# A macaron block on one core: the first and last feed-forward nets in four parts, with weights multiplied ahead

## The chip, the cores and the metric

The kernel runs on one core of a Trainium2 chip. The metric is the device time of one launch, in microseconds (us). TensorE (PE) does products and transposes and has its weight loads listed apart (PEld); VectorE (DVE) and ScalarE (ACT) work on rows of 128 partitions; GpSimd (POOL) is a fourth engine; SyncE's queue (SP) and ScalarE's queue issue the transfers between DRAM and the on-chip memory. Products and transposes end in PSUM, the accumulator memory of eight banks.

## The reference

The input x has 8 chunks of 512 rows and 128 columns, float32. Three steps follow one another, with the same feed-forward weights in the first and the third:

```
x = x + 0.5 * ffn(norm(x))
x = x + attention(norm(x))        # 16 heads, Q and K of rank 64, softmax over 512 rows, VO 128x128 per head
x = x + 0.5 * ffn(norm(x))

def ffn(h):                       # three blocks k = 0, 1, 2
    y = gelu(norm(W1[k] h + b1[k]) * gamma[k] + beta[k])
    h = h + W2[k] y + b2[k]
W = (q / 7.5 - 1) * scale (one scale for 16 columns) + lora_b lora_a     # six matrices of 128x128
norm(v) = (v - mean) / sqrt(var + 1e-5)
```

Softmax runs along the keys, after division of the scores by the root of 128.

## The kernel before

The 512 rows of a chunk lie as four groups of 128 partitions. All matrices of the net are in SBUF, turned (wT). A planner holds the order: `at(t, fn)` files a task with a planned time, tasks are issued in order of that time, and each engine keeps this order exactly. The planned times are written out by hand; T0 is the planned start against the first scores at time 0.

The middle is 32 turns of about 32 us, each of two head pairs of one chunk. A turn computes scores (L624), row maxima (L631), exponentials (L636), the softmax's scaling on POOL and ACT (L648, L650), turns the weights by transposes in 32x32 tiles on DVE (L658) and transfers on SP, and adds the values (L694) into PSUM; projections (L562, L568) and values (L584) of later pairs and the blocks of the feed-forward nets of neighbouring chunks (`Unit`, `Block`: L286, L293, L311, L319, L325) lie between. Here `Norm` takes statistics on DVE (`bn_stats` L250, `bn_aggr` L252), the root on POOL in two instructions (add EPS L258, power −1/2 L259), and z on DVE (L264).

At the head and at the tail one chunk is alone: the first net of chunk 0 with its attention input before the first scores, and the second net of chunk 7 after the last values. `lay_parts` gives each two `Part`s of 256 rows. A part's block has a bias that a product writes to PSUM (L370), two 128-column products with wT (L378), Norm, two transposes (L235), gelu on ACT (L389), the second product (L397) and an addition to h on DVE (L403). HB = 5.5 is the planned time of a block and LAG = 2.55 the offset of the second part. Between the parts `busy` issues transposes that nobody reads (`warm`, L149): 18 at the start, 4 to 6 later, and so on; 12 ahead of the last turn's values, 18 at the tail's start. `lay_last_sum` turns the attention's result (L728, L734) and the last sum (L412) is stored in halves.

Before the head's blocks the loads (L105 to L124), the dequantising of six matrices (`Weights`, L181 to L213: two DVE instructions, the LoRA product and an addition on DVE, transposes and a copy), the columns of biases, gamma and beta (L164), and the transposes of Q and K for all eight pairs (L223) are done. One PSUM pool with banks by tag serves all of it (L66). `g0`, `g1`, `acc0`, `acc1` are one bank each, `scores` two pairs.

Of the kernel before, what the change touches and what calls it, by code (L numbers as in the profile page):

```python
# [18 lines left out]
def kernel(  # L19
# [46 lines left out]
    psum = ctx.enter_context(tc.tile_pool(name="psum", bufs=1, space=bass.MemoryType.PSUM))  # L66
# [9 lines left out]
    vecs = const.tile([P, D], F32, name="vecs")  # L76
    nc.gpsimd.memset(vecs, 0.0)
# [7 lines left out]
    def load_x(b):  # L85
        nc.sync.dma_start(out=xs[b], in_=x[b].rearrange("(p c) d -> p c d", c=NC))

    q_i = const.tile([P, NL, D], I32, name="q_i")
# [3 lines left out]
    la = const.tile([LR, NL, D], F32, name="la")  # L92
    lb = const.tile([P, NL, LR], F32, name="lb")
# [3 lines left out]

    groups = [(0, 2), (2, NL)]

    def load_q(l0, l1):  # L100
        nc.scalar.dma_start(
            out=q_i[:, l0:l1, :], in_=qweights.rearrange("l o d -> o l d")[:, l0:l1, :]
        )

    load_x(0)  # L105
    nc.scalar.dma_start(out=sc, in_=scales.rearrange("l o g -> o l g"))
    load_q(*groups[0])
    nc.sync.dma_start(out=lb, in_=lora_b.rearrange("l o r -> o l r"))
    nc.sync.dma_start(out=la, in_=lora_a.rearrange("l r d -> r l d"))
    load_q(*groups[1])  # L110
    nc.sync.dma_start(out=vecs[0:NL, :], in_=biases)
    nc.sync.dma_start(out=vecs[NL : NL + NB, :], in_=ln_gamma)
    nc.sync.dma_start(out=vecs[NL + NB : NL + 2 * NB, :], in_=ln_beta)
    nc.sync.dma_start(out=q_sb, in_=wq.rearrange("(g two) r d -> (two r) g d", two=2))
    nc.sync.dma_start(out=k_sb, in_=wk.rearrange("(g two) r d -> (two r) g d", two=2))
    nc.scalar.dma_start(
# [3 lines left out]
    load_x(1)  # L120
    load_x(2)
# [38 lines left out]
    cols = const.tile([P, NL + 2 * NB], F32, name="cols")  # L160
    ncol = NL + 2 * NB
    beta_at = NL + NB

    def columns():  # L164
        pt = bank("pt_cols", "g1")
        nc.tensor.transpose(pt[:, 0, :ncol], vecs[:ncol, :], ident[:ncol, :ncol])
        nc.scalar.copy(cols, pt[:, 0, :ncol])


    w = const.tile([P, NL, NG, GROUP], F32, name="w")  # L170
    wf = w.rearrange("p l g k -> p l (g k)")
    lbT = const.tile([LR, NL, P], F32, name="lbT")
    wT = const.tile([P, NL, P], F32, name="wT")

    class Weights:


        def __init__(self, l0, l1):
            self.l0, self.l1, self.n = l0, l1, l1 - l0

        def dequantized(self):  # L181
            l = slice(self.l0, self.l1)
            nc.vector.tensor_scalar(wf[:, l, :], q_i[:, l, :], 1.0 / 7.5, -1.0, ALU.mult, ALU.add)
            nc.vector.tensor_tensor(
                w[:, l], w[:, l],
                sc[:, l, :].unsqueeze(3).to_broadcast([P, self.n, NG, GROUP]), ALU.mult,
            )

        def lora_turn(self):
            self.pt = pt = bank(f"pt_lb{self.l0}", "acc1")  # L190
            for l in range(self.n):
                nc.tensor.transpose(pt[:LR, l, :], lb[:, self.l0 + l, :], ident)

        def lora_keep(self):
            nc.vector.tensor_copy(lbT[:, self.l0 : self.l1, :], self.pt[:LR, : self.n, :])

        def lora(self):
            self.pl = bank(f"pl{self.l0}", "acc1")
            for l in range(self.n):
                nc.tensor.matmul(  # L200
                    self.pl[:, l, :], lhsT=lbT[:, self.l0 + l, :], rhs=la[:, self.l0 + l, :],
                    start=True, stop=True,
                )

        def add(self):
            l = slice(self.l0, self.l1)
            nc.vector.tensor_tensor(wf[:, l, :], wf[:, l, :], self.pl[:, : self.n, :], ALU.add)

        def turn(self):
            pt = bank(f"pt_w{self.l0}", "acc1")  # L210
            for l in range(self.n):
                nc.tensor.transpose(pt[:, l, :], wf[:, self.l0 + l, :], ident)
            nc.scalar.copy(wT[:, self.l0 : self.l1, :], pt[:, : self.n, :])  # L213
# [5 lines left out]
    def projection_weights(src, dst, g0, scale, nm, t, t_keep):  # L219
        def turn():  # L220
            pt = bank(f"pt_{nm}{g0}", "acc1")
            for j in range(NC):
                nc.tensor.transpose(pt[:, j, :], src[:, g0 + j, :], ident)  # L223
            at_keep.append(pt)

        at_keep = []
        at(t, turn)
        at(t_keep, lambda: nc.scalar.mul(dst[:, g0 : g0 + NC, :], at_keep[0], scale))

    def transposed(src, name, tag):  # L230

        n = src.shape[1]
        p = bank(name, tag)
        for c in range(n):
            nc.tensor.transpose(p[:, c, :], src[:, c, :], ident)  # L235
        return p[:, :n, :]

    class Norm:
# [5 lines left out]
        def stats(self):  # L244

            n = self.n = self.src.shape[1]
            st = small.tile([P, NC, 6], F32, tag="st", name=f"st_{self.name}")
            self.mv = small.tile([P, NC, 2], F32, tag="mv", name=f"mv_{self.name}")
            for c in range(n):
                nc.vector.bn_stats(out=st[:, c, :], in_=self.src[:, c, :])  # L250
# [88 lines left out]
    class Part:  # L339
# [13 lines left out]
        def root(self):  # L353
            self.nm.root()
# [627 lines left out]
```

## Time and profile before

| what | us |
|---|---|
| median of three runs | 1098.97 |
| the runs | 1098.64, 1098.97, 1101.04 |
| the profiled execution, its span | 1102.69, 1100.9 |
| first scores (L624) | 35.95 |
| turn starts 0, 1, 2 | 35.95, 68.82, 103.35 |
| end of the last values (L694) | 1071.87 |
| last sum of x, end | 1098.07 |

The chain of waits follows the work that ended last back from the end, each piece with start, length and place; `issue` is time in which the engine waited for nothing visible; rows with ACTq or SPq are queue waits. Windows give the busy time of every engine in a stretch and the clock that the throttle granted to TensorE (1 is full). The profile's mean clock over the run is 0.996. POOL is busy 496.0 us and its adds of EPS take 9.6 us in all (42 with 4 columns, 228 ns each), the powers 128x2 713 ns and 128x4 1029 ns.

### The profile page before, as it was taken

How to read it: one execution, taken by the hardware profiler on the slowest of the kernel's cores; microseconds unless marked ns; L12 is line 12 of the kernel's file. 1: busy time of each engine (PE TensorE's matmuls, PEld its weight loads, DVE VectorE, ACT ScalarE, POOL GpSimd, SP SyncE). 2: the span in 40 equal slices, each digit the busy share in tenths (PEclk: the TensorE clock that was granted, in tenths of full speed). 3: DMA queues.
4: the chain of work that ended last, by engine and by line, in shares of the span. 5: the costliest groups of instructions: out<-in, count | busy, mean ns of one | idle time of the engine just before them, and what ended most of it. 6: DMA issues, size and time to landing. Idle time of an engine off the chain costs nothing.

```text
span 1100.9 us, 15782 instructions
## 1 busy us (share of the span) xinstructions
PE 1074.2 (98%) x4683; PEld 584.6 (53%) x4683; DVE 878.3 (80%) x1772; ACT 787.0 (71%) x1674; POOL 496.0 (45%) x427
## 2 busy tenths in 40 slices
PE   9889999999999999999999999999999999999987
PEld 7546544675555554555555455555445555554445
DVE  6788887878888898888889888888988887777725
ACT  2677787767777777777788777777777777777611
POOL 3453444445444455444445554444544444454402
PEclk9999999999999999999999999999999999999999
DMA  6066555665676545566655556755555665666640
GB/s 183 1 154 146 120 115 122 139 153 131 149 163 134 127 109 120 135 153 153 141 113 120 125 127 151 163 126 125 123 116 135 153 153 125 134 137 150 139 102 10
DMA packets 57291, 142.39 MB, mean 129 GB/s; under 512 B 18348, under 2 KB 22008, under 8 KB 57208
## 3 DMA queue, kind: packets, MB, share of 16 engines
q1 hardware_dynamic: 54840, 139.73, 56.5%
q10 hardware_dynamic: 2368, 1.66, 0.7%
q8 instruction: 39, 0.64, 0.3%
q14 instruction: 44, 0.36, 0.1%
HBM read 5.01 MB, written 2.10 MB: 6 GB/s over the span
## 4 chain that ended last, share of the span: by engine, by line
PE 80%; ACT 9%; DVE 7%; SPq 2%; issue 2%; DMA 1%; POOL 0%; DVEq 0%; ACTq 0%
PE acc L694 33%; PE ps L624 16%; PE pqk L562 9%; PE pv L584 8%; ACT e L636 4%; PE po L319 3%; PE py L286 3%; DVE nm L631 2%; DVE tr L658 2%; SPq L673 2%; PE p L235 2%; ACT e L650 1%; ACT L311 1%; PE warm_acc L149 1%; PE ph L235 1%
## 5 line engine op out<-in xcount | busy, mean ns | idle before, releaser
L648 POOL TENSOR_SCALAR e<-e,rden 128x512 f32<-128x512 f32 x256 | 398.6, 1567 | 331.0 <-DVE rden L643 330.9
L694 PE MATMUL acc<-eT,v 64*128 64x512 f32 (+1 forms) x1768 | 467.2, 590 | 2.3 <-DMA eT<-tr 1.2
L636 ACT ACTIVATE e<-ps,nm 128x512 f32<-128x512 f32 x512 | 345.2, 686 | 162.4 <-DVE nm L631 157.9
L658 DVE STREAM_TRANSPOSE tr<-e 128x1024 f32<-128x1024 f32 x256 | 312.9, 1231 | 34.2 <-POOL e L648 24.4
L631 DVE TENSOR_REDUCE nm<-ps 128x2 f32<-128x1024 f32 x256 | 299.6, 1207 | 50.7 <-PE ps L624 50.3
L694 PEld LDWEIGHTS acc<-eT,v 64*128 64x128 f32 (+1 forms) x1768 | 204.9, 188 | 213.8 <-issue 206.6
L624 PE MATMUL ps<-qk 64*128 64x512 f32 x1024 | 250.8, 599 | 3.4 <-ACT e L636 2.4
L650 ACT ACTIVATE e<-e,rden 128x512 f32<-128x512 f32 x256 | 177.0, 725 | 14.3 <-DVE rden L643 12.9
L624 PEld LDWEIGHTS ps<-qk 64*128 64x128 f32 x1024 | 99.1, 186 | 125.4 <-issue 84.4
L584 PE MATMUL pv<-vo_sb,axT 128*128 128x256 f32 x512 | 122.2, 381 | 0.0
L584 PEld LDWEIGHTS pv<-vo_sb,axT 128*128 128x128 f32 x512 | 95.5, 191 | 27.5 <-issue 14.4
L636 ACT ACTIVATION_READ_ACCUMULATOR e<-ps,nm 128x1 f32 x512 | 103.8, 203 | 0.0
L597 ACT COPY v<-pv 128x512 f32<-128x512 f32 x126 | 68.0, 596 | 47.5 <-PE pv L584 47.5
L258 POOL TENSOR_SCALAR rstd<-mv 128x4 f32<-128x4 f32 x42 | 9.6, 228 | 145.7 <-DVE mv L252 145.7
L643 DVE RECIPROCAL rden<-den 128x2 f32<-128x2 f32 x256 | 40.7, 162 | 36.0 <-ACT e L636 35.0
L562 PE MATMUL pqk<-axT,qT_w 128*128 128x512 f32 x124 | 64.0, 598 | 1.8 <-ACT e L636 1.8
L568 ACT COPY qk<-pqk 128x1024 f32<-128x1024 f32 x62 | 62.1, 1001 | 4.6 <-PE pqk L562 4.6
L562 PE MATMUL pqk<-axT,kT_w 128*128 128x512 f32 x124 | 63.3, 592 | 0.0
L325 DVE SCALAR_TENSOR_TENSOR hT<-po,cols,hT 128x512 f32<-128x512 f32 x42 | 31.0, 739 | 25.0 <-PE po L319 24.1
L286 PEld LDWEIGHTS py<-wT,hT 128*128 128x128 f32 x336 | 43.3, 194 | 13.5 <-DVE hT L325 6.6
L264 DVE TENSOR_SCALAR z<-y,mv,rstd 128x128 f32<-128x128 f32 x168 | 47.9, 354 | 2.1 <-POOL rstd L259 2.1
L293 DVE TENSOR_TENSOR y<-py,bias_bc 128x512 f32<-128x512 f32 x42 | 28.5, 680 | 25.6 <-PE py L286 25.5
(109 smaller groups left out, 769.0 us busy)
## 6 DMA issues: line engine op xcount, KB each, us to landing
eT<-tr SPq DMA_DIRECT2D x1016, 128.0 KB, 2.3
x<-in_L_attn_x_dram SPq DMA_DIRECT2D x8, 256.0 KB, 5.5
out_dram<-x SPq DMA_DIRECT2D x7, 256.0 KB, 2.5
eT<-tr ACTq DMA_DIRECT2D x8, 128.0 KB, 4.2
qk_sb<-in_L_attn_Q_dram SPq DMA_DIRECT2D x1, 512.0 KB, 4.3
qk_sb<-in_L_attn_K_dram SPq DMA_DIRECT2D x1, 512.0 KB, 5.6
q_i<-in_L_ffn_qweights_dram ACTq DMA_DIRECT2D x1, 256.0 KB, 4.8
out_dram<-x SPq DMA_DIRECT2D x2, 128.0 KB, 1.7
```

The costliest lines, as they stand in the source:

```text
L286: nc.tensor.matmul(self.py[:, c, :], lhsT=hTs[self.b][:, c, :], rhs=wT[:, 2 * self.k, :], start=True, stop=True,)
L562: nc.tensor.matmul(self.pg[:, i, :], lhsT=(qT_w, kT_w)[i][:, self.g, :], rhs=xTs[self.b], start=True, stop=True,)
L568: nc.scalar.copy(self.qk, self.pg)
L584: nc.tensor.matmul(p, lhsT=xTs[self.b][:, c, :], rhs=vo_sb[:, 2 * self.g : 2 * self.g + 2, :], start=True, stop=True,)
L597: nc.scalar.copy(self.v[:, c : c + NC // 2], self.pv[:, c : c + NC // 2])
L624: nc.tensor.matmul(ps[:, j, :], lhsT=self.qk[rows, 0, ts(c, P)], rhs=self.qk[rows, 1, :], start=True, stop=True,)
L631: nc.vector.tensor_reduce(self.nm[:, c, :], self.ps[c], AX.X, ALU.max, negate=True)
L636: nc.scalar.activation(e[:, j, :], self.ps[c][:, j, :], AF.Exp, bias=self.nm[:, c, j : j + 1], accum_out=self.den[:, c, j : j + 1],)
L648: nc.gpsimd.tensor_scalar(e, e, r, None, ALU.mult)
L650: nc.scalar.activation(e, e, AF.Copy, scale=r)
L658: nc.vector.transpose(self.tr[:, :, :, c, :], self.e[c].rearrange("p h (k j r) -> p j (h k) r", j=Q4, r=32),)
L694: nc.tensor.matmul(accs[self.b][i], lhsT=self.v[rows, k, j, :], rhs=self.eT[rows, :, j * NC + k, :], start=first, stop=end and (j == 1 or ...
```

## The change

The two ends are laid out anew; the plan of the middle is the same except where named.

- **PSUM** comes from three pools in turn, "start", "attention" and "end". In the ends each of the four parts has a bank of its own for the sums of its three blocks and the final one (`y0` to `y3`), and a quarter of a bank for transposes.
- **Four parts** of 128 rows replace two of 256. Biases enter PSUM by transposing a broadcast column. Statistics of each part are a `bn_stats` and a `bn_aggr` whose input holds a constant third entry D·EPS, so the root is one POOL instruction; the middle's Norm uses the same form.
- **Weights multiplied ahead**: W1[k]·W2[m] is made once (`natural`, `multiplied`), so the pre-activation of block k is a sum in PSUM of W1[k]·h0, and of products with the earlier blocks' gelu outputs. In the tail no second product, no h and no addition remain between blocks; in the head the first block keeps them (`second`, `second_add`), and later ones don't. `constants` puts the earlier blocks' biases in.
- **`busy` transposes**: left are 14 at the start and eight at each of four places of turn 0 (times 5.3, 10.4, 15.6, 31.9); those between the parts, the 12 before the last values and the 18 at the tail's start are gone.
- **Weights**: scale first divided by 7.5 (`sc75`), then one DVE instruction for dequantising; LoRA is added in PSUM by TensorE.
- **Loads** come in another order and in pieces, over both queues. Q and K of pair 0 are turned at the head; pairs 1 to 3 and 4 to 7 in turn 0, along with two of the multiplied weights. The Exp table is loaded at time 0.01, after the first scores, and the eight `busy` before turn 1 use bank acc0.
- **Rings**: y two instead of three buffers (the attention copy `a` shares them), aT two instead of three in Block, hT three instead of four.
- **The last stores** are four, one a part, on SP and ACT.

```diff
-    psum = ctx.enter_context(tc.tile_pool(name="psum", bufs=1, space=bass.MemoryType.PSUM))
+    class Psum:
+        def __init__(self):
+            self.names, self.stack = ["start", "attention", "end"], ExitStack()
+        def next(self):
+            self.stack.close()
+            self.tile = self.stack.enter_context(tc.tile_pool(
+                name=f"psum_{self.names.pop(0)}", bufs=1, space=bass.MemoryType.PSUM,
+                reuse_waits="tile",
+            )).tile
...
+    sts = const.tile([P, 6, NC, 9], F32, name="sts")
+    nc.gpsimd.memset(sts, 0.0)
+    nc.gpsimd.memset(sts[:, :, :, 8:9], D * EPS)
...
+    load_lb(0)
+    load_q(0, 1, nc.scalar)
+    load_x(0, 0, 2)
     nc.scalar.dma_start(out=sc, in_=scales.rearrange("l o g -> o l g"))
+    load_la(0, nc.scalar)
+    nc.sync.dma_start(out=bias_rows, in_=biases)
+    load_x(0, 2, NC)
+    load_q(1, G, nc.scalar)
+    load_lb(1)
+    nc.sync.dma_start(out=gb_rows[0:NB, :], in_=ln_gamma)
+    nc.sync.dma_start(out=gb_rows[NB : 2 * NB, :], in_=ln_beta)
+    load_la(1, nc.sync)
+    load_q(G, NL, nc.sync)
+    load_projections(0, 1)
+    load_x(1)
+    load_projections(1, HP)
+    load_x(2)
...
+    def dequantized(l0, l1):
+        i, n = l0 // G, l1 - l0
+        nc.vector.scalar_tensor_tensor(
+            w[i][:, l0 - G * i : l1 - G * i],
+            q_i[:, l0:l1, :].rearrange("p l (g k) -> p l g k", k=GROUP), -7.5,
+            sc75[:, l0:l1, :].unsqueeze(3).to_broadcast([P, n, NG, GROUP]), ALU.add, ALU.mult,
+        )
...
+    def weights(l0, l1, tag):
+        i, n = l0 // G, l1 - l0
+        pt = bank(f"pt_w{l0}", tag)
+        for l in range(n):
+            nc.tensor.matmul(
+                pt[:, l, :], lhsT=w[i].rearrange("p l g k -> p l (g k)")[:, l0 - G * i + l, :],
+                rhs=ident, is_transpose=True, start=l == 0, stop=False,
+            )
+        for l in range(n):
+            nc.tensor.matmul(
+                pt[:, l, :], lhsT=la[i][:, l0 - G * i + l, :], rhs=lbT[i][:, l0 - G * i + l, :],
+                start=False, stop=l == n - 1,
+            )
+        return lambda: nc.scalar.copy(wT[:, l0:l1, :], pt[:, :n, :])
...
+    def natural(m, tag):
+        pt = bank(f"pt_nat{m}", tag)
+        nc.tensor.transpose(pt[:, 0, :], wT[:, 2 * m + 1, :], ident)
+        return lambda: nc.scalar.copy(nat[:, m, :], pt[:, 0, :])
+    def multiplied(ks, m, tag):
+        pt = bank(f"pt_x{ks[0]}{m}", tag)
+        x = const.tile([P, len(ks), P], F32, name=f"wx{ks[0]}{m}")
+        for i, k in enumerate(ks):
+            nc.tensor.matmul(
+                pt[:, i, :], lhsT=nat[:, m, :], rhs=wT[:, 2 * k, :], start=True, stop=True
+            )
+            wX[k, m] = x[:, i, :]
+        return lambda: nc.scalar.copy(x, pt[:, : len(ks), :])
...
+        for i, (k, m) in enumerate(((2, 1), (1, 0), (2, 0))):
+            nc.tensor.matmul(
+                pt[:, 0, i : i + 1], lhsT=wT[:, 2 * k, :], rhs=col[2 * m + 1],
+                start=i == 0, stop=i == 2,
+            )
...
-            st = small.tile([P, NC, 6], F32, tag="st", name=f"st_{self.name}")
+            norms.append(self.name)
+            st = sts[:, NC + len(norms) % 2]
...
-            nc.gpsimd.tensor_scalar(rstd[:, :n], self.mv[:, :n, 1], EPS, None, ALU.add)
-            nc.gpsimd.tensor_tensor(rstd[:, :n], rstd[:, :n], mhalf[:, :n], ALU.pow)
+            nc.gpsimd.tensor_tensor(rstd[:, :n], self.mv[:, :n, 1], mhalf[:, :n], ALU.pow)
...
-            y = work.tile([P, NC, D], F32, tag="y", name=f"y{self.name}")
+            y = work.tile([P, NC, D], F32, tag="y", name=f"y{self.name}", bufs=2)
...
-            self.aT = work.tile([P, NC, P], F32, tag="aT", name=f"aT{self.name}")
+            self.aT = work.tile([P, NC, P], F32, tag="aT", name=f"aT{self.name}", bufs=2)
...
-        hTs[b] = work.tile([P, NC, P], F32, tag="hT", name=f"hT{f}_{b}", bufs=4)
+        hTs[b] = work.tile([P, NC, P], F32, tag="hT", name=f"hT{f}_{b}", bufs=3)
...
+        def stats(self, k=None):
+            self.src = self.x() if k is None else self.y[:, k, :]
+            nc.vector.bn_stats(out=sts[:, self.c, 0, 0:6], in_=self.src)
+        def mean(self):
+            self.mv = small.tile([P, 2], F32, tag="pmv", name=f"pmv{self.name}")
+            nc.vector.bn_aggr(out=self.mv, in_=sts[:, self.c, 0, :])
         def root(self):
+            self.rstd = small.tile([P, 1], F32, tag="prstd", name=f"prstd{self.name}")
+            nc.gpsimd.tensor_tensor(self.rstd, self.mv[:, 1:2], mhalf[:, 0:1], ALU.pow)
...
+        def to_y(self, k, lhsT, rhs, end=False, turn=None):
+            nc.tensor.matmul(
+                self.y[:, k, :] if isinstance(k, int) else self.y[:, k[0] : k[1], :],
+                lhsT=lhsT, rhs=rhs, is_transpose=turn, start=bool(k == 0 and turn), stop=end,
+                skip_group_check=True,
+            )
         def bias(self, k):
+            b = col[2 * k] if k <= self.known else consts[self.known][k]
+            self.to_y(k, b.to_broadcast([P, P]), ident, turn=True)
+        def input(self, k, k1=None):
+            if k == NB:
+                self.to_y(k, self.h, ident, turn=True)
+            elif k1 is None:
+                self.to_y(k, self.h, wT[:, 2 * k, :], end=k <= self.known)
+            else:
+                self.to_y((k, k1), self.h, wT[:, 2 * k : 2 * k1 - 1 : 2, :])
+        def of_block(self, k, m):
+            self.to_y(
+                k, self.g[m], wX[k, m] if k < NB else wT[:, 2 * m + 1, :],
+                end=m == min(k, NB) - 1,
...
+        def second(self, k):
             nc.tensor.matmul(
+                self.p[1], lhsT=wT[:, 2 * k + 1, :], rhs=self.g[k], start=True, stop=True
+            )
+        def second_add(self, k):
+            h = self.h
             nc.vector.scalar_tensor_tensor(
+                self.new_h(), self.p[1], col[2 * k + 1], h, ALU.add, ALU.add
...
+    def part_banks(f):
+        ys = [bank(f"py{f}_{i}", f"y{i}") for i in range(NC)]
+        p = [bank(f"pp{f}_{i}", f"g{i}") for i in range(2)]
+        return [(ys[i], [p[i % 2][:, 2 * (i // 2) + j, :] for j in range(2)]) for i in range(NC)]
...
-        a.append(work.tile([P, T], F32, tag="a", name=f"a{b}", bufs=1))
+        a.append(work.tile([P, T], F32, tag="y", name=f"a{b}", bufs=2))
...
-    T0 = -33.0
...
+    T0 = -23.98
+    t = {k: T0 + v for k, v in START.items() if isinstance(v, float)}
     at(T0 + 0.1, table, AF.Gelu)
     at(T0 + 1.4, idle_bank, "acc0")
+    at(T0 + 1.5, busy, 14)
...
+        (t["qt"], t["qtk"], q_sb, qT_w, 0, 1, 1.0 / math.sqrt(D), "acc0"),
+        (t["kt"], t["ktk"], k_sb, kT_w, 0, 1, 1.0, "acc1"),
+        (0.4, 0.6, q_sb, qT_w, 1, 4, 1.0 / math.sqrt(D), "acc1"),
+        (1.4, 1.5, k_sb, kT_w, 1, 4, 1.0, "g1"),
+        (20.0, 24.3, q_sb, qT_w, 4, HP, 1.0 / math.sqrt(D), "acc1"),
+        (24.6, 28.4, k_sb, kT_w, 4, HP, 1.0, "acc1"),
+    ):
+        projection_weights(src, dst, g0, g1, scale, tag, ta, tb)
+    lay(20.1, 24.2, natural, 0, "acc0")
+    lay(24.5, 28.3, multiplied, (1, 2), 0, "acc0")
...
+    at(0.0, psum.next)
+    at(0.01, table, AF.Exp)
+    at(0.3, idle_bank, "acc0")
+    at(31.8, idle_bank, "acc0")
+    for t in (5.3, 10.4, 15.6, 31.9):
         at(t, busy, 8)
...
-    at(t + 25.8, idle_bank, "scores")
-    at(t + 25.9, busy, 12)
...
-    at(E + 1.65, idle_bank, "acc1")
-    at(E + 1.7, busy, 18)
...
+    for m in lay_parts(1, B - 1, 0, E, END, end_banks, (
+        ("xadd", "attended"), ("start", "start"), ("y0", "input", 0), ("in12", "input", 1, NB),
+        ("y1", "of_block", 1, 0), ("o20", "of_block", 2, 0), ("y2", "of_block", 2, 1),
+        ("in3", "input", 3), ("o30", "of_block", 3, 0), ("o31", "of_block", 3, 1),
+        ("o32", "of_block", 3, 2),
+    )):
```

## The prediction, made before the result was known

> **What bounds the kernel now.** I read the section of busy shares first, then the chain of waits over the whole span, then its pieces at both ends, then windows for the granted clock.
>
> ```profile
> PE 1074.2 (98%) x4683; PEld 584.6 (53%) x4683; DVE 878.3 (80%) x1772; ACT 787.0 (71%) x1674; POOL 496.0 (45%) x427
> PE 80%; ACT 9%; DVE 7%; SPq 2%; issue 2%; DMA 1%; POOL 0%; DVEq 0%; ACTq 0%
> ```
>
> TensorE bounds the middle: the 32 turns run from the first scores (L624, 35.95) to the end of the last L694 (1071.87). At the ends its 98% is misleading, because fillers (L149) count as busy. The ends hold 35.95 + (1100.9 − 1071.87 = 29.0) = 65 us, in which one chunk's feed-forward net runs with nothing beside it. So the change must be read from the ends, and from what it leaves in the turns.
>
> ```profile
> 1086.41 0.57 ACT aT L389
> 1086.98 0.04 issue
> 1087.02 0.70 PE po L397 x2
> 1087.72 0.43 PE py L370 x2
> 1088.15 0.22 PE warm_acc L149 x2
> 1088.37 0.64 PE py L378 x4
> 1089.01 0.27 PE p_b L235 x2
> 1089.28 0.02 issue
> 1089.30 0.02 ACTq L389
> 1089.32 0.05 issue
> 1089.36 0.57 ACT aT L389
> 1089.94 0.04 issue
> 1089.98 0.70 PE po L397 x2
> ...
> 1097.17 0.45 PE ph L235 x2
> 1097.63 0.02 issue
> 1097.65 0.42 DVE x L412
> ```
>
> The chain of waits, tail: two halves alternate, 2.96 us each, so a block takes 5.92. Of each 2.96 TensorE works 2.26 in its written order (second product, bias, filler, first product, the other half's transposes) and waits 0.70 for the gelu. The root on POOL is covered by the other half. The last sum ends at 1098.07, 26.2 after the last L694; the store and the span's end take 2.83 more.
>
> ```profile
> 43.49:46.90 3.41, 1.57 (x9) 0.58 (x6) 2.75 (x4) 2.86 (x7) 2.80 (x3) 1.00 0.02 5
> 46.90:50.31 3.41, 3.41 (x13) 2.94 (x14) 3.12 (x7) 1.14 (x4) 2.52 (x2) 0.50 0.00 0
> 60.55:63.97 3.42, 1.65 (x6) 0.75 (x5) 3.42 (x5) 2.79 (x8) 0.61 (x2) 1.00 0.80 175
> 1057.25:1060.66 3.41, 1.25 (x7) 0.70 (x7) 1.61 (x10) 0.00 (x0) 1.26 (x2) 1.00 0.16 35
> 1060.66:1064.07 3.41, 3.41 (x15) 2.89 (x14) 0.00 (x0) 0.78 (x1) 0.00 (x0) 0.50 0.00 0
> ```
>
> Windows: length, busy PE, PEld, DVE, ACT, POOL, then the clock. The clock's edges lie 3.41 us apart or a multiple of it (5.94, 46.90, 50.31, 1060.66, 1064.07). The step after one with TensorE 1.57 (46%) or 1.25 us busy (37%) ran at half clock; 60.55, with 1.65 (48%), kept the full clock after it.
>
> **The change, part by part.** I laid the instructions of both ends, old and new, on each engine in its written order with the durations of the rows (below: the adding-up): product of 128 columns 0.38 alone (0.215 each in a row); transpose 0.33; statistics 0.28 and their mean 0.15; pow 128x2 0.71 and 128x4 1.03, so 128x1 about 0.55 (by extension); z 0.34; ACT copy 256 0.37 and 512 0.59, so 128 about 0.27; gelu 256 0.56 and 512 0.78, so 128 about 0.46; sums 256 0.42, so 128 about 0.31; handover 0.02 to 0.04, to POOL 0.08.
>
> *Tail.* From block 0 on, second product (0.70), its add (0.50), bias (0.43) and fillers leave the chain; the EPS add on POOL (0.23) too. One part needs per block: product 0.38, statistics 0.43, handover 0.08, pow 0.55, z 0.34, transpose 0.33, gelu 0.46, handovers 0.25 = 2.8. Four parts share VectorE, which per block does 4 x (0.28 + 0.15 + 0.34) = 3.1 us. The larger decides: 3.2 against 5.92. Before the blocks: copy of the result 0.27, transpose with the 16 bias transposes among them (16 x 0.107 = 1.7, beside VectorE), then four parts through x add, statistics, mean, z at 1.05 each: the last z ends about 5.0 after L694, transpose, copy and product bring its first pre-activation to 6.2. Three periods of 3.2 less the product already counted, the last product 0.43 and sum 0.31: 6.2 + 9.6 + 0.7 = 16.4. The same adding-up of the old tail gives 24.3 where the rows have 26.2, so I stretch by 1.08: 17.7. The store (a quarter of the rows, on its own queue) stays at 2.8. Gain 8.5. Bounds: if the parts' sharing is as bad as today's halves (TensorE in its order), the period is 4.0 and the gain 6.1; if the plan holds unstretched, 10.
>
> *Head.* The first pre-activation cannot start before scales, weights, LoRA and x. Old row: 8.78. New: LoRA-B first, 14 warmers at the half clock end 4.7, its three transposes to 5.8, copy, W0, copy: 7.8. The landings of the new order are unseen; nearest rows are x0 3.73, scales 4.14, lb 5.11, la 5.85, so 7.5 to 9.3; I take 7.8. ACT issues four loads (0.5 each) ahead of its table load, which ends at 4.1, before its first copy. On SP, Q and K of pair 0 stand behind the last three weights; their transposes come at 10.0 in TensorE's order, where the old Q landed at 9.76 and K at 11.5: 0 to 1.5, I take 0, since a piece is an eighth of a load. Chunk 1's x (old 12.2) is first read at 22. Block 0 is slowed by turning five more weights between (TensorE 10.0 to 12.0 waits twice for an ACT copy of wT, 0.5 each) and keeps its second product; then blocks of 3.3. The last sum of x comes at 22.1 by this adding-up. There the order hurts: chunk 1's four statistics and means (1.07 on VectorE) and its 128x4 pow (1.03 on POOL) are ahead of the last part's root, and its z is at 25.9 instead of 23.5. Transpose 0.33, copy 0.27, K product and the remaining Q: scores at 27.8. The same adding-up gives 33.5 for the old 35.95; gain 5.7 x 1.07 = 6.0. From 21 to 26 TensorE is busy 42 to 44% of any 3.4 us by the same adding-up, below the 46% at which the clock fell, so I expect the next 3.4 us at half clock: projections and first scores (1.15 alone at full) cost 1.0 more (0 to 2). Net 5.0. Bounds 2 and 9 (the plan's own order without chunk 1's insertion, 2.4 better).
>
> *The first two turns.* Five further Q/K weight transposes and two sets in turn 0: 0.5 on TensorE. The Exp table (1.28, L142) now comes after the last copies and largely fits under scores 1.15 + maximum 1.24; 0.3 is left. The eight warmers before turn 1 use bank acc0 and wait for the copy of the last multiplied weights, behind v copies on ACT: 1.6. Turn 1 had 0.6 of issue (70.83) waiting for eT, absorbed by a later start. Sum +1.8 (0.5 to 4).
>
> *The last turn.* Twelve fillers (2.49 at half clock) go; eT had landed at about 1058.8, so L694 starts after the transposes of 1059.70 (x4). The stretch at half clock follows the hole anyway. I take −1.3 (0 to −2.5).
>
> *Turns 2 to 30.* One instruction less per Norm (L258, 0.23 on POOL, which waits 145.7 us for its inputs and mostly off the chain), smaller rings for y, aT, hT. Nothing on TensorE changes. Cover: TensorE is busy 98%; without it each of 42 roots would give 0.3. I take 0, bounds −3 and +3.
>
> Sum against the profiled execution's 1102.69: −8.5 − 5.0 + 1.8 − 1.3 = −13.0, 1089.7. The three runs' median is 3.7 lower, so 1086.0.
>
> **A rule that speaks against it.** The rows above put the edge between 46 and 48% of a step. The Trainium skill, "TensorE: Matmul & The Clock Gate", Part 1, says the clock halves after an idle free-running window of 3413 ns; the trace's steps agree in length, but its windows were not idle. Its Part 4 says that the full clock does not engage for transposes; here the first 18 fillers are transposes and the clock was full from 5.94, so the trace decides. By Part 4's rule the bare tail, with half its TensorE work transposes, would lose the clock often: an estimate from that page is 4 us more, 1090.
>
> **The rivals.**
> *Clock lost in the ends (about 1091).* If two steps of the tail and one more of the head run at half clock, products and transposes on the chain (0.38 + 0.33 per 2.8 us) take twice as long and the four parts queue on TensorE: about 1.7 a step, 5 more. For it: short records with waits between them; how much of a record counts as work is unseen. Against: by the same adding-up the tail keeps TensorE at 75% or more, until its last sums.
> *The head gains nothing (about 1091).* If scales or the last three weights land 2 us late, or the turn-0 work grows to 4, only the tail's 8.5 less the extras is left.
> *The order holds as planned (about 1081).* Chunk 1's root falls elsewhere and no clock is lost: 4 to 5 better.
> *Slower than before (about 1104).* Rings of two y (shared with the attention copy), two aT, three hT: a bias add on VectorE (L293) that waits for a ring's old reader stands before the row maxima, and so before the exponentials. It decides from 13/31 = 0.42 us a turn; at 0.6 a turn it is +18.6 − 13, +5.6. For it: VectorE is 80% busy. Against: TensorE's idle time before L624 and L694 is 3.4 and 2.3 us in all, and DVE's waits for POOL 24.4.
> *The ends stay under another bound (no change, 1098).* The old tail's chain has no DMA in it, so I see no cover.
>
> **How the numbers follow.** Forecast 0.58; clock 0.14; head without gain 0.11; order as planned 0.09; slower 0.06; no change 0.02. The likeliest gives 1086.0. Its bounds by terms, mostly independent, are about ±4; the two weaker cases reach 1092, the better 1081. Range 1080.5 to 1092.5. A measurement of this kernel tells 0.2% (2.2 us) from no change: faster 0.92, same 0.02, slower 0.06.
>
> **What would show it.** Right: first scores near 29, last sum about 18 after the last attention product, part blocks about 3.3 apart; turn 1 starting about 35 after turn 0; a granted clock of 0.5 around the first scores; 30 middle turns within 0.05 us of before. Wrong: block period near 4 or a tail at half clock; the first pre-activation after 9; a wait in every turn for y or hT.

## The result, and the profile after

The changed kernel takes 1086.23 us (median of four runs, 1085.0 to 1087.01) beside 1099.11 for the kernel before (four runs); the ratio of the runs is 0.9878, with a 95% interval of 0.9861 to 0.9896 (the two medians give 0.9883). The forecast was 1086.0. The profiled execution took 1085.0, its span is 1083.2.

The stages of the two profiled executions, from the first scores' start, the starts of each turn's first row maximum, the end of the last values and the span's end (from the first scores to the first row maximum both take 1.18, which no row holds):

| stage | before | after | difference | forecast |
|---|---|---|---|---|
| to the first scores | 35.95 | 29.58 | −6.4 | −5.0 |
| turns 0 and 1 | 67.40 | 68.33 | +0.9 | +1.8 |
| turns 2 to 30 | 916.7 | 915.8 | −0.9 | 0 |
| last turn, to the end of the values | 50.63 | 48.28 | −2.35 | −1.3 |
| tail | 29.0 | 20.06 | −8.9 | −8.5 |
| span | 1100.9 | 1083.2 | −17.7 | −13.0 |

The spans differ by 17.7, the medians by 12.9. The profiled execution of before was 3.6 above its median, that of after 1.2 below. Of this scatter 1.2 lies in turns 3, 5, 6 and 23, which had 0.2 to 0.4 more in the one profile of before and show both values in later profiles of its variants (turn 3 31.38 and 31.03, turn 23 33.29 and 32.94). Turn 0 may hold another 0.9: it took 33.27 in the one profile of before, 32.31 and 32.45 in two variants of it with the same head and turn 0. Where the rest lies was not found. So the total agrees to 0.2 us, but the terms below add up to 4.7 more than the forecast, and its carry-over from profile to median hid that.

Section 1 of the page of after, the busy shares:

```profile
PE 1061.0 (98%) x4630; PEld 563.4 (52%) x4630; DVE 874.5 (81%) x1765; ACT 795.0 (73%) x1710; POOL 484.5 (45%) x367
```

Nothing here tells the gain: TensorE has the same share, and only 53 instructions less. The chain of waits does. The tail of after, with start, length and piece:

```profile
1063.19 0.28 ACT oT L1103
...
1068.30 0.28 ACT ph L469
1068.57 0.04 issue
1068.61 1.15 PE py L473 x6
1069.76 0.41 PE pp L462 x2
...
1079.16 1.11 PE py L473 x6
...
1080.29 0.29 DVE end L523
```

Where TensorE waited 0.70 of each 2.96 us for a gelu, there is one unbroken run of TensorE from 1068.61 to 1080.27. Each piece is products and transposes of whichever part is due; no gelu, root or addition stands in the chain. The first part's gelus start at 1069.91, 1073.49 and 1076.86: a block takes 3.4 to 3.6, where it took 5.92. The last sum ends 17.4 after the last values (before 26.2).

The head's end in after, the same view:

```profile
23.63 0.29 DVE x L523
23.93 0.78 DVE sts L336 x4
24.70 0.30 DVE mv_n L338 x4
...
25.87 1.01 POOL rstd_n L344
26.88 0.52 POOL prstd L453
...
27.43 0.36 DVE pz L457
```

L336, L338 and L344 are chunk 1's statistics and root; they stand on VectorE and on POOL ahead of the last part of chunk 0, whose z (L457) is the last thing the projections need.

### The profile page after: what moved, and what is told of

Read it like the earlier page. It is cut to its first block, busy times and chain, and to the rows that moved or that the text cites. A ratio compares the mean times of both kernels' runs of the same rounds, so it can differ in the third digit from the quotient of the medians.

```text
span 1083.2 us, 15632 instructions
## 1 busy us (share of the span) xinstructions
PE 1061.0 (98%) x4630; PEld 563.4 (52%) x4630; DVE 874.5 (81%) x1765; ACT 795.0 (73%) x1710; POOL 484.5 (45%) x367
## 4 chain that ended last, share of the span: by engine, by line
PE 79%; ACT 9%; DVE 8%; issue 2%; SPq 1%; POOL 1%; DMA 0%; DVEq 0%; ACTq 0%; POOLq 0%
PE acc L792 33%; PE ps L722 16%; PE pv L682 9%; PE pqk L659 8%; ACT e L734 5%; PE po L403 4%; DVE tr L756 3%; PE py L371 3%; DVE nm L729 3%; PE py L473 2%; PE p L318 2%; SPq L771 1%; ACT e L748 1%; ACT L396 1%; ACT v L695 1%
## 5 line engine op out<-in xcount | busy, mean ns | idle before, releaser
L792 PEld LDWEIGHTS acc<-eT,v 64*128 64x128 f32 (+1 forms) x1768 | 196.9, 188 | 219.1 <-issue 216.5
L722 PEld LDWEIGHTS ps<-qk 64*128 64x128 f32 x1024 | 94.6, 186 | 127.9 <-issue 89.9
L344 POOL TENSOR_TENSOR rstd<-mv,mhalf 128x4 f32<-128x4 f32 x42 | 43.0, 1024 | 150.9 <-DVE mv L338 150.9
L695 ACT COPY v<-pv 128x512 f32<-128x512 f32 x126 | 68.0, 596 | 46.9 <-PE pv L682 46.8
```

Source lines behind the costliest of these rows:

```text
L695: nc.scalar.copy(self.v[:, c : c + NC // 2], self.pv[:, c : c + NC // 2])
L722: nc.tensor.matmul(ps[:, j, :], lhsT=self.qk[rows, 0, ts(c, P)], rhs=self.qk[rows, 1, :], start=True, stop=True,)
L792: nc.tensor.matmul(accs[self.b][i], lhsT=self.v[rows, k, j, :], rhs=self.eT[rows, :, j * NC + k, :], start=first, stop=end and (j == 1 or ...
```

## The experiments

All ratios are to the kernel before, run beside each; 0.9878 is the changed kernel's. Beside the experiments the kernel before took 1100.3 to 1100.7 (medians of 9 to 19 runs), 1.2 to 1.6 above its 1099.11 beside the changed kernel, which was not run again. So a ratio compared with 0.9878 can be off by 0.001 to 0.0015 from this alone, and what a part is worth is read from the stages of the profiles. In what follows a step is one of the stretches of 3.41 us at whose ends the granted clock can change, and a half step is one at half clock.

### Chunk 1's statistics earlier

```diff
-    m.lay_start((-3.3, -2.9, -1.6, 1.95, 3.7), "g0")
+    m.lay_start((-13.05, -13.0, -1.6, 1.95, 3.7), "g0")
```

> The changed kernel with chunk 1's statistics and root planned at -13.05 and -13.0 instead of -3.3 and -2.9, so that they no longer stand before the last part's root. Theory (the insertion costs the head its place): in the changed kernel the last part's z starts at 27.43, after 1.2 us of chunk 1's statistics on VectorE and 1.01 us of its power on POOL; without them 25.0, so first scores 29.6 - 2.3 = 27.3 and the time 2 us shorter (1 to 2.5), less what the moved 1.2 us on VectorE cost block 1 of the parts (0 to 0.5). Rival (TensorE or ACT is the bound there anyway): first scores move less than 0.5.

Ratio 0.9853 (0.9821 to 0.9886), which overlaps the changed kernel's interval; three runs took 1080.91 to 1083.17, one 1089.31. The last z starts at 25.76 instead of 27.43 and the first scores at 27.96 instead of 29.58. So the insertion cost the head 1.6 us. 2.3 was expected; 0.4 of the difference is that the parts' last sum came later (24.06 instead of 23.63), and the clock also rose 0.4 later (5.28 instead of 4.85).

### Q and K of pairs 1 to 3 turned in the head

```diff
-        (0.4, 0.6, q_sb, qT_w, 1, 4, 1.0 / math.sqrt(D), "acc1"),
-        (1.4, 1.5, k_sb, kT_w, 1, 4, 1.0, "g1"),
+        (T0 + 20.5, T0 + 20.6, q_sb, qT_w, 1, 4, 1.0 / math.sqrt(D), "acc0"),
+        (T0 + 20.7, T0 + 20.8, k_sb, kT_w, 1, 4, 1.0, "acc1"),
```

> The changed kernel with the Q and K transposes of pairs 1 to 3 and their copies at 20.5 to 20.8 of the head's plan instead of behind the first scores. Theory (turn 0 lost 1.1 us to them): in the changed kernel ACT's copy of K waits for transposes queued behind the second scores and the first exponentials start at 33.15, 1.16 after the maximum they need ended; then turn 0 gets shorter by 1.1 and the first scores stay at 29.6 (0 to 0.3 later). Rival (turn 0 is bound by chunk 1's first block or the values): turn 0 shorter by less than 0.4.

What it was about, in the timeline of after (start, length, engine, line, work, and the idle time before it with what ended it):

```profile
30.76 1.23 DVE L729 TENSOR_REDUCE nm<-ps 128x2 f32<-128x1024 f32 x1 [0.88 <-PE ps L722]
...
32.18 0.55 PE L308 MATMUL pt_g<-ident,qk_sb 128*128 128x128 f32 x3
...
32.76 0.49 ACT L311 ACTIVATE kT_w<-pt_g 128x384 f32<-128x384 f32 x1 [0.70 <-PE pt_g L308]
33.15 0.68 ACT L734 ACTIVATE e<-ps,nm 128x512 f32<-128x512 f32 x1
```

The maximum is ready at 31.99. The first exponential stands behind a copy that stands behind transposes that stand behind the second scores: 1.16 us lost, and not by the Exp table, which had ended at 31.46. With the transposes moved the exponential starts with the maximum's end:

```profile
34.16 0.69 ACT L734 ACTIVATE e<-ps,nm 128x512 f32<-128x512 f32 x1 [0.34 <-DVE nm L729]
```

Turn 0 is 33.43; the fair comparison is the profile with chunk 1's statistics moved, 34.55, since both ran it at full clock: 1.1 shorter, as expected. The ratio is 0.9835 (0.9816 to 0.9854). The median moved by more than 1.1 (1082.51 against 1086.23). The mean granted clock of the four executions is 1.000, that of the changed kernel's 0.997 to 0.998, so the half steps of after are missing here; whether the move or chance kept them out is not shown. And this profiled execution began late: its first scores are at 31.73, for a reason that the run with fillers in the holes shows.

### The tail of before in the changed kernel

```diff
-    at(E + 0.01, psum.next)
...
-    for m in lay_parts(1, B - 1, 0, E, END, end_banks, (
...
+    at(t + 25.8, idle_bank, "scores")
+    at(t + 25.9, busy, 12)
+    lay_last_sum(B - 1, E, ((0.9, 1.4), (1.0, 2.4)))
+    lay_old_parts(
+        1, B - 1, [[E + t for t in times] for times in (
+            (1.8, 3.7, 4.2, 4.6, 1.5), (2.8, 4.8, 5.3, 5.7, 1.6)
+        )],
...
+    at(E + 1.65, idle_bank, "acc1")
+    at(E + 1.7, busy, 18)
```

> The changed kernel with the tail of before: two parts of 256 rows with second products and additions, the fillers between them, 18 at its start and 12 before the last values; only the root is one instruction as elsewhere in the changed kernel. Theory (the ends are independent): the last turn 2.35 longer, as in before, the tail 9.0 longer less 3 to 4 roots of 0.3 on the chain: 8 to 9, together 10.5 to 11.5 us slower than the changed kernel. Rival (part of the tail's gain came from the state in which the turns leave it): under 8.

Ratio 0.9979 (0.995 to 1.0008): 0.0101 above the changed kernel's, 11.1 us, as expected. Five runs took 1096.04 to 1097.42 and one 1106.13, which pulls the ratio up; the medians differ by 10.6. The tail and the end of the last turn are worth most of the change, and apart from the rest. Inside this profile the tail is 32.12, not 29.0; a half step fell on it from 1065.87, and the clock fell again at 1089.77. Its last turn, with the twelve fillers and at full clock, takes 47.91; with chunk 1's statistics moved, without them and at full clock, 46.91. So the twelve cost 1.0, and a half step in that turn the other 1.4 (48.28 in after).

### The kernel before without its fillers in the ends

```diff
-                if i == 0:
-                    for dt, n in ((0.6, 3), (2.0, 2), (3.4, idle[k]), (4.9, 2)):
-                        at(t + dt, busy, n)
...
-    for t in (26.6, 28.0, 29.9, 30.8):
-        at(T0 + t, busy, 6)
...
-    at(t + 25.9, busy, 12)
...
-    at(E + 1.7, busy, 18)
```

> The kernel before without the fillers between the parts of both ends, without the 12 before the last values and the 18 in the tail; the first 18 and 4 stay. Theory (the fillers cost little between blocks, since TensorE waits 0.70 of each 2.96 anyway; the chain runs over them with 0.22 each): last turn 1 to 2.5 shorter, tail 1.5 to 3 shorter, head 1 to 3 shorter, 4 to 7 us faster in all, with the clock at full. Rival (the fillers hold the clock): steps at half clock in the ends, and no gain or a loss.

Ratio 0.9993 (0.9983 to 1.0002): the expectation failed and its rival held in the tail. In the profile the head is 0.9 shorter, turn 0 1.6 and the last turn 3.5 (these two without the half steps that before had there), but the tail is 2.2 longer. The runs show no gain: this profile is of the fastest of its ten executions (1098.31), and that of before is of one 3.6 above its median. Windows of its tail, with length, busy PE, PEld, DVE, ACT, POOL, the clock, DMA share and GB/s:

```profile
1069.24:1072.66 3.42, 2.00 (x12) 1.35 (x11) 1.78 (x9) 0.74 (x2) 1.28 (x3) 1.00 0.00 0
1072.66:1076.07 3.41, 2.06 (x5) 1.53 (x6) 1.70 (x8) 0.56 (x1) 0.93 (x2) 0.50 0.00 0
1076.07:1079.48 3.41, 3.41 (x12) 2.59 (x10) 1.39 (x6) 0.56 (x1) 0.50 (x2) 0.50 0.00 0
```

With two parts and no fillers TensorE is busy 58% of the step from 1069.24 and loses the clock for the next two. So taking the fillers out is not what gained: it is affordable with four parts, which keep TensorE busy by themselves.

### A tail of four parts without the multiplied weights

```diff
-    for m in lay_parts(1, B - 1, 0, E, END, end_banks, (
-        ("xadd", "attended"), ("start", "start"), ("y0", "input", 0), ("in12", "input", 1, NB),
-        ("y1", "of_block", 1, 0), ("o20", "of_block", 2, 0), ("y2", "of_block", 2, 1),
...
+    for m in lay_parts(1, B - 1, 2, E, END, end_banks, (
+        ("xadd", "attended"), ("start", "start"), ("y0", "input", 0),
+        ("second0", "second", 0), ("sadd0", "second_add", 0), ("y1", "input", 1),
+        ("second1", "second", 1), ("sadd1", "second_add", 1), ("y2", "input", 2),
...
```

> The changed kernel with a tail of four parts that does not use the multiplied weights: blocks 0 and 1 have a second product, its addition to h on VectorE, and the last sum comes from h. Theory (the period is VectorE's share or the chain, whichever is longer): two more products and additions on the chain, 2 x 0.8 to 1.0, and VectorE's share of a block 4.3 instead of 3.1, so the tail is 1.6 to 3 longer: most of the tail's 9.0 belongs to the four parts without fillers. Rival (the multiplied weights bring most of it): 4 or more.

Ratio 0.9893 (0.987 to 0.9917), the tail 23.0 against 20.06: 2.9 longer, within the expectation. By these two profiles, of the tail's 8.9 the multiplied weights bring 2.9 and the four parts with all else 6.0; the runs (1086.37 to 1091.63) do not tell the two kernels apart by their ratios. The planned times of this tail were only shifted to make room, so a better order might lose less. The chain shows what they remove; it has VectorE's additions in it again:

```profile
1071.68 0.36 DVE ph L515
...
1072.61 0.30 DVE sts L445
```

### The loads in the order of before

```diff
-    load_lb(0)
-    load_q(0, 1, nc.scalar)
-    load_x(0, 0, 2)
+    load_x(0)
     nc.scalar.dma_start(out=sc, in_=scales.rearrange("l o g -> o l g"))
-    load_la(0, nc.scalar)
+    load_q(0, 2, nc.scalar)
+    load_lb(0)
+    load_lb(1)
...
```

> The changed kernel with the loads in the order of before, x of chunk 0 whole first, weights 0 and 1 together, LoRA-B after x, the last four weights on ACT's queue, Q and K whole. Theory (the head starts with LoRA-B's transposes and weights 0, and both come later): the first pre-activation 0.7 to 1.5 later (7.69 in the changed kernel), first scores 0.5 to 2 later. Rival (TensorE's order in blocks 0 and 1 is the bound): first scores later by less than 0.3.

The profile has the first pre-activation at 10.06 instead of 7.69 and the first scores at 33.06 instead of 29.58, more than expected; but two half steps fell into this head (8.40 to 11.81 and 28.88 to 32.29). The ratio, 0.988 (0.9862 to 0.9898), cannot be told from the changed kernel's. What the order is worth in the median stays open.

### Both moves, and fillers put into TensorE's holes

```diff
+    at(9.4, busy, 14)
...
+    at(t + 13.3, idle_bank, "scores")
+    at(t + 13.4, busy, 20)
```

The first kernel has the two moves above, the second also these lines.

> The two moves together (chunk 1's statistics early, the Q and K transposes of pairs 1 to 3 in the head). Theory (two separate causes): first scores near 28.0 where the clock rises by 5.3, turn 0 near 33.4, so 1.6 and 1.1 to 2.1 better than the changed kernel, ratio to the kernel before near 0.983 or below. Rival (both free the same wait): no better than the better one alone, 0.9835.

> The two moves and 34 fillers put into two holes of TensorE: 14 in turn 0 before the first product of chunk 2's net (TensorE waits there 1.8 us for a copy), 20 before the last net's transposes in the last turn (TensorE waits 3.5 us there). Theory (a step at half clock follows a step with a hole, when the free-running step falls on it, and costs 1.0 in turn 0 and 1.4 in the last turn): no step at half clock in the profile, last turn 46.9 in every profile, median 1 to 2 lower than with both moves alone and a smaller spread. Rival (the chain passes over the fillers, or the holes shrink): the same or up to 1 slower.

Both moves: 0.9839 (0.9822 to 0.9857). The first scores are at 28.09, and the first exponential starts with its maximum's end (30.53 and 30.50), so each did its part in the profile. Yet the time is not better than with the Q and K move alone (0.9835). This profile has a half step in turn 0, which takes 34.44 where that one took 33.43, and one in the last turn (48.30 against 46.94); that one had neither. The two intervals do not separate them.

Fillers in the holes: 0.9853 (0.9827 to 0.9878), medians 1082.80 against 1083.17 with both moves alone: no gain that the runs tell. In the profile neither turn has a half step. Turn 0 takes 33.42, 1.0 less than with both moves alone, and the last turn 47.50, 0.8 less; 46.9 was expected there, so the fillers lengthened it by 0.6. The two holes are gone there, but the run with the Q and K move had no half step either, with its holes, so one profile does not show that the fillers are the cause. A half step fell on the tail instead, from 1071.18 (21.28 against 20.05). This run showed more in its head. It is the same program up to the first scores, and they came at 34.55 instead of 28.09. The chain of the head, first of the run with both moves and the fillers, then of after, at the same work:

```profile
1.55 3.26 PE warm_acc L189 x14
...
14.46 0.64 PE pt_w L237 x3
```

```profile
1.56 3.26 PE warm_acc L189 x14
...
10.79 0.33 PE pt_w L237 x3
```

The opening fillers take 0.23 each in both, half clock. Then after's transposes take 0.11 each, the other's 0.21: there the granted clock rose at 23.28, in after at 4.85. (The windows view prints 1.00 ahead of the first recorded rise, so the durations must be read.) Two of its five executions took 1088.23 and 1087.57, the other three 1082.28 to 1082.8; the profiled one is the 1088.23.

### Seven fillers at the start, and twenty

```diff
-    at(T0 + 1.5, busy, 14)
+    at(T0 + 1.5, busy, 7)
```

The second kernel has both moves and 20.

> The changed kernel with 7 instead of 14 fillers at its start. Theory (the clock rises only after a free-running step of 3.41 us that TensorE fills, and the bare head hardly fills one by itself at half clock): in the profiles so far steps at half clock with 1664 to 2048 columns of work were followed by full clock in most cases and steps with 1158 to 1670 were not; with 7 fillers no opening step is filled, so the clock rises at 9 or later, the first scores come 3 to 7 us later than 29.6 and the median is 3 to 6 above the changed kernel (ratio to before 0.990 to 0.994). Rival (the next step is filled anyway by products at half clock): first scores at most 1 later, ratio 0.988 or lower, since 7 fillers less end 1.5 us earlier.

> Both moves with 20 instead of 14 fillers at the start, which end 1.3 us later. Theory (a filled opening step is made sure): the profile has the full clock by 6.5, first scores 28.0 + 0.7 to 1.3, no execution more than 3 us above the others, median 0.5 to 1.2 above both moves alone (0.9839). Rival (14 are enough and the slow executions have another cause): still executions 5 us above the others.

With seven: 0.9896 (0.9865 to 0.9927), 2.0 above the changed kernel by the ratios, 2.8 by the medians, and less than expected; the runs are 1085.51, 1086.59, 1091.5 and 1091.79. The profiled one (1086.59) has the rise at 9.90 and the first scores at 31.14, 1.6 later; a half step from 26.97 is in that. So the rise can come from the head's own work. Two of four runs about 5 us above the others suggest that fewer fillers make a late rise likelier; when the clock rose in those two was not seen. With twenty: rise at 6.32, first scores 29.14 (1.05 after those with 14), 0.9839 (0.982 to 0.9858), runs 1080.94 to 1084.24. No execution stood out, but among four that shows little, since with 14 none of five did in the run with both moves either.

### The smaller rings, and the root without the addition, in the kernel before

```diff
-            y = work.tile([P, NC, D], F32, tag="y", name=f"y{self.name}")
+            y = work.tile([P, NC, D], F32, tag="y", name=f"y{self.name}", bufs=2)
...
-        hTs[b] = work.tile([P, NC, P], F32, tag="hT", name=f"hT{f}_{b}", bufs=4)
+        hTs[b] = work.tile([P, NC, P], F32, tag="hT", name=f"hT{f}_{b}", bufs=3)
```

```diff
-            nc.gpsimd.tensor_scalar(rstd[:, :n], self.mv[:, :n, 1], EPS, None, ALU.add)
-            nc.gpsimd.tensor_tensor(rstd[:, :n], rstd[:, :n], mhalf[:, :n], ALU.pow)
+            nc.gpsimd.tensor_tensor(rstd[:, :n], self.mv[:, :n, 1], mhalf[:, :n], ALU.pow)
```

> The kernel before with the smaller rings of the change alone: y two, shared with the attention copy, aT two, hT three. Theory (the rings cost nothing, and the changed turns 1, 3 and 23 have another cause): every turn from 2 to 30 as in the kernel before within 0.05 (except single half-clock steps), ratio within 0.998 to 1.002. Rival (a ring's wait in every turn): 0.2 to 0.6 a turn, 6 to 18 us slower.

> The kernel before with the instruction that adds EPS on POOL left out (the norm is taken without EPS). Theory (in the turns the root is covered; in the ends two halves cover each other's roots; only the first and last roots of an end lie bare): turns 2 to 30 within 0.05 apart from turns 1, 3 and 23, which lose 0.4 to 1.3 as in the changed kernel if the root is their cause; ends 0.3 to 1.5 shorter; 1 to 4 us faster, ratio 0.996 to 0.999. Rival (every root lies on the chain): 42 x 0.3 = 12 us faster.

Rings: 0.9997 (0.9986 to 1.0007); turns 2 to 30 as in the kernel before, apart from single turns 0.2 to 0.35 off that differ from profile to profile. The rings cost nothing. The root without its addition: 0.9989 (0.9975 to 1.0002), tail 28.68 instead of 29.0. 1 to 4 us were expected; the interval holds no gain as well, and excludes the rival's 12. In the turns it is covered. Turn 1 stays at 34.1 and 34.6 in these two, where every kernel with the new head has 32.8 to 33.3, so turn 1's gain is not theirs; by exclusion it belongs to the head and turn 0.

## Why the prediction was right, point by point

**The total.** That it agrees to 0.2 us is luck. All five terms came out better than forecast, by 4.7 together (17.7 against 13.0); the forecast then took off 3.7 for before's slow profile, and the profile of after lies 1.2 below its own median. What was right is the mechanism: the gain lies in the tail, the head and the last turn, with little else moved.

**The tail** (8.5 forecast, 8.9 measured). Right in size; the step that failed is what sets the period. "Four parts share VectorE ... 3.1 us. The larger decides: 3.2" — the chain shows TensorE in one piece, 3.4 to 3.6 a block. From 1066 to 1080 TensorE is busy 13.1 of 14 us and VectorE 11.0. I had added up VectorE's share and one part's chain, but not TensorE's: a part has six products with gelu outputs, one of 128 and one of 256 columns with h, h's transpose and three of z, 6 x 0.215 + 0.215 + 0.43 + 4 x 0.107 = 2.4 us of bare issue in its three blocks, 9.4 for the four, in one written order. That is less than the 11.7 us of the unbroken run, so short waits lie hidden under the records' ends. The trace names what ended them: of the 76 records of the run six start 0.04 us after a gelu and five 0.04 us after a z, and these waits, with the wider spacing of the record behind each, make 1.9 us. So TensorE's own work, 3.1 a block, is no less than VectorE's 3.1, and in its one written order it also waits for the parts; no run took work from one of the two engines alone. The sum 6.2 + 9.6 + 0.7 is 16.5, not 16.4; stretched by 1.08 its blocks of 3.2 are 3.5, which happened to cover the wait. That second products and additions leave the chain was right: 2.9 by the run without them.

**The head** (6.0 less 1.0 for the clock; 6.4 measured). The first pre-activation at 7.8 (7.69), the insertion of chunk 1 (1.6, argued at 2.4) and the scores at 27.8 x 1.07 = 29.7 (29.58) held. The 1.0 for a half step, and with it the sign of a granted clock of 0.5 around the first scores, did not come in this execution: TensorE was busy 49% of the step from 21.92 and kept the clock. (The sign "first scores near 29" leaves that 1.0 out; the forecast's own sum puts them at 35.95 − 5.0 = 30.95.) In two other profiles with this head, those with the old loads and with seven fillers, such a half step did fall there. No run tells apart what the four parts, the multiplied weights and the shorter dequantising are worth in the head.

**The first two turns** (1.8; 0.9). Turn 0 lost 2.25 (3.1 against the two later variants of before), but not where I put it. The wait for the multiplied weights' copy was 0.56, not 1.6; the Exp table cost nothing; the copy of K ahead of the first exponential cost 1.1, which I had taken for part of 0.3. What else turn 0 lost is not shown. Turn 1 gave back 1.3, not 0.6.

**The last turn** (−1.3; −2.35). I took half of the fillers as covered. The runs at full clock put 1.0 on the fillers in the changed kernel (47.91 and 46.91) and 2.0 in the kernel before (49.14 without the addition of EPS, 47.14 without fillers). A half step lies in before's 50.63 and in after's 48.28, as forecast, but this differs from profile to profile.

**Turns 2 to 30** (0; −0.9). Right: rings and root cost and gain nothing there; the 0.9 is the scatter of before's one profile.

**The clock.** "The rows above put the edge between 46 and 48% of a step" fell. Steps with TensorE 43 to 45% busy kept the full clock (the kernel before without fillers, 1052.2; chunk 1's statistics moved, 1046.3; the old loads, 1052.9), and a step with 84% was followed by the half clock (the old tail, 1062.46). The same hole of the last turn shows it best, first in after, then with chunk 1's statistics moved:

```profile
1049.33:1052.74 3.41, 1.55 (x6) 0.52 (x4) 2.22 (x13) 0.00 (x0) 1.03 (x1) 1.00 0.61 159
1052.74:1056.16 3.42, 3.42 (x7) 1.56 (x7) 0.16 (x1) 0.78 (x1) 0.00 (x0) 0.50 0.00 0
```

```profile
1046.30:1049.70 3.40, 1.54 (x5) 0.48 (x3) 2.21 (x12) 0.00 (x0) 1.03 (x1) 1.00 0.67 180
1049.70:1053.10 3.40, 3.31 (x10) 1.67 (x10) 0.49 (x2) 0.78 (x1) 0.00 (x0) 1.00 0.00 0
```

The share of a step alone is not what decides. The Trainium skill, "TensorE: Matmul & The Clock Gate", Part 1, calls for an idle window ahead of a fall; the steps ahead of the falls here held 37 to 84% of work, so that the rule, taken by the recorded steps, does not fit either. Where in the step the hole lies does matter (the last section); the whole rule was not found. Of the rivals, "clock lost in the ends" is half true: it did not bind in this profile, but the head's rise differs from execution to execution, at a price of 6.5 in the one late rise that was profiled beside an early one (34.55 against 28.09).

**The slower rival**, rings waiting in each turn, is excluded by the run of the rings in the kernel before.

## What to carry to other kernels

Ask of filler work what else could keep the engine busy: two halves without fillers gained nothing that the runs tell, and their tail lost 2.2 at half clock; four parts without fillers, with all else of the new tail, gained 6. A small copy or transpose moved out of a lone stage into a busy one must be followed through both queues: here an ACT copy behind TensorE's second scores held up the first exponential by 1.1 us. If times scatter between two values, look at the first microseconds: a clock that rises one or five steps later moves the whole program.

The two moves beat both kernels, by more than the 0.0015 that the kernel before moved between the comparisons: 0.9835 with Q and K turned in the head, 0.9839 with chunk 1's statistics early as well, against 0.9878.

## What the runs showed of the hardware

The granted clock changes only at points 3.41 us apart, but these lie anywhere against the program: the first rise came at 4.33, 4.43, 4.85, 4.99, 5.28, 5.59, 10.74 and 23.28 in heads that open with the same 14 fillers. At half clock a transpose of 128 columns takes 0.213, so by the columns of the matmul records a step at half clock can hold 2048. Steps with 1664 to 1792 were followed by a rise in most profiles, and steps with 1792 at 6.2 and 13.0 were not in the execution that rose at 23.28. A head whose chain leaves TensorE small gaps may so stay at half clock by its own slowness; this is a reading of the one execution.

Half steps cost 1.4 in the last turn (48.28 against 46.91) and 1.0 in turn 0 (35.52 against 34.55; with the Q and K move 34.44 against 33.43). Whether one comes there depends on where the steps lie against the program. In the last turn of the changed kernel and its variants the records leave TensorE idle for 1.86 us at one place, 12.7 before the end of the last values in after. The half clock followed in the three profiles in which this hole began 0.97 to 1.11 after a step's start, and not in the six in which it began 1.30 to 2.31 after it. The hole of 1.84 us in turn 0 was followed by it in the ten profiles in which it began 0.40 to 1.41 after a step's start, and not in the three in which it began 2.04 to 2.63 after it, so that the step's end cut it.
